# Layer 3's context attention and relative attention as one stage of a Perceiver kernel

## The chip, the core and the metric

The kernel runs on one core of a Trainium2 chip. TensorE (PE) multiplies matrices, VectorE (DVE), ScalarE (ACT) and GpSimd (POOL) work on vectors, and SyncE (SP) issues most DMA transfers. Each engine has its own instruction queue. The metric is the time of one execution in device microseconds. In the profile PE and PEld stand for TensorE's matmuls and weight loads. A float32 matmul appears as two rows of the profile, so a group "x4" is two matmuls.

## The reference, cut to what matters

The whole network is four layers on `x` (2 batches, 256 positions, 256 channels) with a context of 2 x 4096 rows. The change touches two consecutive sublayers of the last layer, each with 16 heads of depth 16 and a residual:

```python
def _L3_xattn_ref(q, kv, mem, w_q, w_kv, w_concat):    # q = layernorm(x), mem = kv = context
    c = jnp.concatenate([mem, kv], axis=1)
    qh = (q @ w_q).reshape(B, L, N_HEAD, D_HEAD).transpose(0, 2, 1, 3)
    kvp = c @ w_kv
    k, v = (kvp[..., :D_HEAD], kvp[..., D_HEAD:])
    attn_score = jnp.einsum('bhid,bjd->bhij', qh, k) / np.sqrt(D_HEAD)
    attn_prob = jax.nn.softmax(attn_score, axis=-1)
    out = jnp.einsum('bhij,bjd->bhid', attn_prob, v)
    return out.transpose(0, 2, 1, 3).reshape(B, L, D) @ w_concat

def _L3_attn_ref(x, gamma, beta, Wq, Wk, Wv, Wr, u_bias, v_bias, Wo, bo, rel_pos_emb):
    xn = (x - mu) * jax.lax.rsqrt(var + EPS) * gamma + beta     # of an x that is normed already
    q, k, v = heads(xn @ Wq), heads(xn @ Wk), heads(xn @ Wv)
    r = (r_emb @ Wr).reshape(2 * L - 1, NUM_HEADS, DEPTH).transpose(1, 0, 2)
    AC = jnp.einsum('bhld,bhmd->bhlm', q + u_bias[None, :, None, :], k)
    BD = jnp.einsum('bhld,hrd->bhlr', q + v_bias[None, :, None, :], r)
    score = (AC + _rel_shift(BD)) / jnp.sqrt(jnp.float32(DEPTH))
    out = jnp.einsum('bhlm,bhmd->bhld', jax.nn.softmax(score, axis=-1), v)
    return out.transpose(0, 2, 1, 3).reshape(B, L, D_MODEL) @ Wo + bo

x = x + _L3_xattn_ref(_layernorm(x), ctx_1024, ctx_1024, ...)
x = x + _L3_attn_ref(_layernorm(x), ...)
```

Batches do not mix in either sublayer. The second sublayer's batch b needs only the first sublayer's batch b, and `r` depends on no activations at all.

## The kernel before

Tokens are held as four tiles of 128 rows (`NT` = 4); tiles 0 and 1 are batch 0, tiles 2 and 3 batch 1. Four heads of 32 rows (16 used, one row for the maximum or the denominator) stand in the 128 partitions of one column block, so a matmul on one head uses 32 rows of the array, and matmuls of different heads can run side by side.

**Context attention, `l3_xattn`.** Work goes in eight groups, one for each token tile and half of the heads; batch 0 is groups 1 to 4, batch 1 groups 5 to 8. A group has 16 rounds over the 4096 context rows. In a round `weights` (L2446 on) makes the scores of the group's heads against 256 context rows (eight matmuls, L2454) and their exponentials on ACT (four instructions, L2458). Two heads that share 32 rows of the array stand side by side in the columns; such a pair fills one bank and is called a head where banks are counted. `weigh` (L2464 on) multiplies the exponentials of the round before with the values (eight matmuls, L2470) and adds the result to a running sum. Beside them `maxima` (L2418 on) makes the row maxima of the next group (matmuls L2430, reductions on DVE L2434). The maxima run two rounds ahead, so the last 18 rounds (two of group 7 and all 16 of group 8) have none; there the sums are added by DVE (L2475) and not by ACT and POOL. The first group's maxima are made ahead of everything by `four_at_once` (the "quads", L2411 and L2415).

PSUM has eight banks. In this stage a pool gives four to the tag "mm" and four to "tr"; a tag's banks are reused in turn. In the last 18 rounds `weights` takes two heads' banks from "tr" and two from "mm", and `weigh` one from "tr".

At the end of a group `back` (L2483 on) turns the sums, divides by the denominator and writes `z`. After the last group all of `z` is transposed, multiplied with the output weight and added to `x`.

**Relative attention, `l3_attn`.** First comes `rT` (relative embeddings times their weight, eight matmuls of 512 columns), then the norm of the norm, a transpose with gamma and beta, and the front: `query` (a matmul pair per batch and column block, with two biases, L2568 and L2569), `key`, `values`. Work then goes in eight units u, one for each token tile and half of the heads. `relative(u)` makes q times r (eight matmuls of 384 columns in four steps of a pair, L2599), copies it to `bd`, writes `bd` to DRAM and reads it back skewed into `bd_shift` (L2604, L2609). `weights(u)` makes the content scores, four turns of two matmuls (L2624), adds the shifted part and finds the maximum on DVE (L2628), and takes exponentials on ACT (L2632). `turned(u)` transposes the result (L2642), `weigh(u)` multiplies with the values (L2655). Round u holds `relative(u + 3)`, `weights(u)`, `turned(u - 1)` and `weigh(u - 2)`, a step of each in turn; `relative` of units 0 to 2 stands ahead of the rounds with queries and keys.

**The order.** `in_order` (L339 on) ties the instructions of the named engines to the order in which the program issues them: PE, DVE and ACT in `l3_xattn`; PE, DVE, ACT and SP in `l3_attn`. Other engines and the parts outside are placed by the scheduler. Weights come through a ring of four buffers.

## Time and profile before

Three runs took 2503.56, 2503.85 and 2503.92 us (median 2503.85). The profiled execution took 2507.48 us, its span from first to last instruction is 2505.7 us, mean granted clock 0.981.

| stretch of the profiled execution, us | what runs | length, us |
|---|---|---|
| 1837 to 1857 | last keys, layer norm, transposes, query projection of the context attention | 20 |
| 1857 to 1893 | maxima of the first group, four heads at once | 36 |
| 1893 to 2229 | rounds with maxima of the next group, 48 us a group | 336 |
| 2229 to 2267.5 | 18 rounds without maxima | 38.4 |
| 2267.5 to 2309 | last sums, output projection, rT, norms, front of the relative attention | 41.5 |
| 2309 to 2382 | rounds of the relative attention | 73 |
| 2382 to 2393 | output projection, start of the feed-forward sublayer | 11 |
| 2393 to 2506 | feed-forward sublayer with experts | 113 |

Rows of the timeline give a start, a length, the engine, the line, what is written and read with the tile sizes, the number of instructions merged into the row, and in brackets how long the engine had been idle and what ended that. Rows of windows give the window, its length, the busy time and instruction count of each engine, the granted clock of PE as a share of the full one, the share of DMA busy time and the GB/s moved. The span of a pipelined PE row is modelled at its end, so starts of successive rows are the surer measure.

### The profile page before, as it was taken

What the parts mean: (1) busy time and instruction counts of PE and PEld (TensorE: products, weight loads), DVE (VectorE), ACT (ScalarE), POOL (GpSimd) and SP (SyncE); (2) the same over time, 40 slices, a digit from 0 to 9 for tenths busy, and PEclk for the clock granted to TensorE, in tenths of its full rate; (3) what the DMA queues carried; (4) which work ended last, traced back from release to release, by engine and by line L of the source; (5) the groups of instructions that cost most, each with busy time, mean ns of one, the idle gap of its engine ahead of it and who ended that gap; (6) DMA issues with size and microseconds to landing.
All of it is one profiled execution on the core that took longest, in us unless ns stands there. A gap on an engine that the chain in (4) does not pass through costs nothing.

```text
span 2505.7 us, 51321 instructions
## 1 busy us (share of the span) xinstructions
PE 2413.6 (96%) x20499; PEld 1612.5 (64%) x20501; DVE 1691.5 (68%) x3077; ACT 1347.7 (54%) x2556; POOL 912.1 (36%) x856
## 2 busy tenths in 40 slices
PE   8999999999999999999899998999989999999989
PEld 6865477777766666666633465556945666665678
DVE  5555588888877777777669755544268888854642
ACT  3334576666666666666466422432215777785612
POOL 0420066666666666665539412001011222210010
PEclk9999999999999999999999999999988999999989
DMA  8221433333342222222410102125840000003656
GB/s 301 97 95 68 141 99 97 98 98 94 99 130 70 69 70 72 70 69 69 137 49 1 68 22 93 60 76 193 312 152 1 2 2 2 2 2 121 235 238 217
DMA packets 92638, 243.60 MB, mean 97 GB/s; under 512 B 8072, under 2 KB 23248, under 8 KB 81904
## 3 DMA queue, kind: packets, MB, share of 16 engines
q1 hardware_dynamic: 81088, 219.08, 26.2%
q10 hardware_dynamic: 8784, 13.24, 1.4%
q0 software_dynamic: 2528, 8.00, 0.9%
q8 instruction: 162, 2.65, 0.4%
q14 instruction: 76, 0.62, 0.1%
HBM read 206.87 MB, written 33.42 MB: 96 GB/s over the span
## 4 chain that ended last, share of the span: by engine, by line
PE 90%; DVE 5%; ACT 2%; DMA 1%; issue 1%; POOL 0%; SPq 0%; DVEq 0%; ACTq 0%; POOLq 0%
PE ps_tr L1238 15%; PE ps_mm L359 14%; PE ps_mm L1285 10%; PE acc L1332 9%; PE ps_tr L2470 5%; PE ps_mm L2430 5%; PE ps_tr L2454 5%; PE acc L359 3%; PE ps_tr L359 2%; PE acc L563 2%; PE acc L1618 2%; PE ps_mm L823 2%; PE ps_mm L1238 2%; PE ps_tr L839 2%; PE ps_tr L921 2%; DVE mx L2415 1%
## 5 line engine op out<-in xcount | busy, mean ns | idle before, releaser
L1320 POOL TENSOR_TENSOR total<-total,S 128x512 f32<-128x512 f32 x434 | 543.1, 1283 | 227.4 <-ACT S L1309 226.9
L1309 ACT ACTIVATE S<-S 128x512 f32<-128x512 f32 x512 | 304.1, 626 | 209.2 <-DVE S L1306 209.0
L1295 DVE TENSOR_TENSOR most<-ps_mm,most 128x512 f32<-128x512 f32 x448 | 278.1, 683 | 101.1 <-ACT S L1292 101.1
L1306 DVE TENSOR_TENSOR S<-S,ps_dec 128x512 f32<-128x512 f32 x512 | 317.2, 677 | 1.7 <-PE ps_dec L1367 1.7
L2434 DVE TENSOR_REDUCE mx<-ps_mm 128x1 f32<-128x512 f32 x448 | 278.1, 683 | 51.4 <-PE ps_tr L2454 48.2
L1292 ACT COPY S<-ps_mm 128x512 f32<-128x512 f32 x512 | 262.4, 598 | 73.3 <-PE ps_mm L1285 73.1
L2458 ACT ACTIVATE PT<-ps_tr 128x512 f32<-128x512 f32 x476 | 246.7, 601 | 81.7 <-PE ps_tr L2454 79.2
L1238 PEld LDWEIGHTS ps_tr<-w_l1x_wv,ctxT 128*64 128x64 f32 x4096 | 235.5, 137 | 46.3 <-issue 41.7
L1285 PE MATMUL ps_mm<-qT,kT 64*128 64x256 f32 x2048 | 256.6, 389 | 0.7 <-DVE qT L1244 0.7
L1332 PE MATMUL acc<-S,v 128*64 128x256 f32 x2048 | 252.2, 385 | 1.7 <-ACT S L1309 1.0
L1238 PE MATMUL ps_tr<-w_l1x_wv,ctxT 128*64 128x128 f32 x4096 | 248.3, 273 | 0.0
L2454 PE MATMUL ps_tr<-qm,kT 32*128 32x256 f32 x1904 | 239.7, 390 | 0.0
L2430 PE MATMUL ps_mm<-kT,qT 32*128 32x512 f32 x896 | 228.3, 625 | 3.4 <-DVE mx L2415 3.3
L1285 PEld LDWEIGHTS ps_mm<-qT,kT 64*128 64x128 f32 x2048 | 188.5, 186 | 44.5 <-issue 12.2
L1332 PEld LDWEIGHTS acc<-S,v 128*64 128x64 f32 x2048 | 139.5, 136 | 96.3 <-ACT S L1292 33.8
L1238 PE MATMUL ps_tr<-ctxT,w_l1x_wk 128*64 128x512 f32 x800 | 189.6, 593 | 0.0
L2454 PEld LDWEIGHTS ps_tr<-qm,kT 32*128 32x128 f32 x1904 | 172.0, 185 | 16.5 <-issue 6.2
L2479 POOL TENSOR_TENSOR sums<-sums,part 128x256 f32<-128x256 f32 x102 | 73.9, 724 | 249.7 <-ACT part L2478 249.7
L2470 PE MATMUL ps_tr<-PT,v 128*32 128x256 f32 x2048 | 139.4, 385 | 0.0
L2430 PEld LDWEIGHTS ps_mm<-kT,qT 32*128 32x128 f32 x896 | 80.2, 187 | 48.4 <-issue 41.1
L336 DVE COPY v<-ps_tr 128x512 f32<-128x512 f32 x120 | 82.4, 687 | 42.5 <-PE ps_tr L1238 42.5
L1238 PEld LDWEIGHTS ps_tr<-ctxT,w_l1x_wk 128*64 128x64 f32 x800 | 59.7, 137 | 70.5 <-issue 58.9
(582 smaller groups left out, 3845.5 us busy)
## 6 DMA issues: line engine op xcount, KB each, us to landing
ctxT<-in_ctxT SPq DMA_DIRECT2D x144, 512.0 KB, 3.6
w_l2f_gu<-in_l2f_gu SPq DMA_DIRECT2D x16, 1024.0 KB, 7.2
bd_dram<-bd SPq DMA_DIRECT2D x8, 1536.0 KB, 6.5
w_l3f_w<-in_l3f_w SPq DMA_DIRECT2D x11, 1028.0 KB, 8.2
w_l3f_w<-in_l3f_w SPq DMA_DIRECT2D x11, 1024.0 KB, 5.4
ctxT<-in_ctxT SPq DMA_DIRECT2D x8, 1024.0 KB, 7.0
ctx<-in_ctx SPq DMA_DIRECT2D x8, 1024.0 KB, 4.8
ahead_ctx<-in_ctxT SPq DMA_DIRECT2D x8, 1024.0 KB, 7.0
```

Of the source, the lines that this page charges most:

```text
L359: self.nc.tensor.matmul(out, lhsT, rhs, start=i == 0, stop=i == len(pairs) - 1)
L1238: nc.tensor.matmul(ps[part], a[:, part], b, start=k == 0, stop=k == len(pairs) - 1)
L1285: nc.tensor.matmul(banks[hh, i][:, j, :], k[part, ts(2 * i + j, P)], q[u][part, :], start=True, stop=True)
L1295: nc.vector.tensor_tensor(m, ps, m, ALU.max)
L1306: nc.vector.tensor_tensor(t, t, spread[u][:, hh, :].unsqueeze(1).to_broadcast([P, 2, L]), ALU.add)
L1309: nc.scalar.activation(t, t, AF.Exp)
L1320: nc.gpsimd.tensor_add(tot, tot, t)
L1332: nc.tensor.matmul(av[u][part], vs[:, 2 * i + j, part], got[hh, i][:, j, :], start=g % 8 == 0 and i + j == 0, stop=g % 8 == 7 and i + j == 2,)
L2430: nc.tensor.matmul(ps, qT[rows, 2 * half + c, ts(t, P)], kT[rows, ts(j, 512)], start=True, stop=True,)
L2434: nc.vector.tensor_reduce(mx[:, c, r, j : j + 1], ps, AX.X, ALU.max)
L2454: nc.tensor.matmul(ps[:, i, :], kT[rows, ts(2 * u + i, P)], q[rows], start=True, stop=True)
L2470: nc.tensor.matmul(ps[ts(r, 32), :], v[:, 2 * u + i, :], pt[:, i, :], start=i == 0, stop=i == 1)
```

## The change

Both sublayers become one function, `l3_attention`, with the same arithmetic save for the reciprocal square roots of the second norm, which POOL computes as a power of -0.5 in place of ACT's square root and DVE's reciprocal.

- `rT` is made at the start, after the layer norm is issued and ahead of the transposes of its result on PE.
- `in_order` covers PE, DVE, ACT, POOL and SP over both attentions.
- In the last 18 rounds of the context attention PSUM is divided anew: three "mm" banks, four "tr", one "acc". All four heads of `weights` take "tr", `weigh` takes "mm". Each of these rounds also takes two steps of `first_front`: batch 0's output projection and norms (`entered`), its queries, relatives 0 and 1, keys and values, with all copies on DVE. Its 22 steps are used up in 11 rounds.
- The weights for that are loaded, and buffers for it are opened in the memory of batch 0's context keys, at group 5, round 3.
- The rounds of the second attention begin at once after the last group. `second_front` (38 steps: relatives 2 to 7 and batch 1's `entered`, queries, keys and values) runs in rounds 0 to 3, two or three steps for each of the four turns of a round.
- `PT` of the context attention has 14 buffers in place of 16; a relative's write and read-back are issued one directly after the other.

```diff
+        rT = front.tile([P, 4, NT * P], F32, name="rT")
+        with self.in_order(e.PE, e.Activation):
+            for c in range(4):
+                ps = self.bank([P, NT * P])
+                self.mm(ps, [(wr[:, k, ts(c, P)], rel[:, k, :]) for k in range(KC)])
+                nc.scalar.copy(rT[:, c, :], ps)
+            xnT = self.to_T(xn)
...
-            def weigh(t, half, u, pts, vector):
-                ps = self.bank([P, 256], "tr")
+        def weigh(t, half, u, pts, more):
+            ps = self.bank([P, 256], "tr" if more else "mm")
...
+        def power(var, eps, name):
+            v, r = (front.tile([P, 2], F32, name=f"{n}_{name}", tag=f"{n}_{name}", bufs=2) for n in ("var", "pow"))
+            nc.vector.tensor_scalar_add(v, var, eps)
+            nc.gpsimd.tensor_tensor(r, v, minus_half, ALU.pow)
+            return r
+        def entered(b):
+            zT = turn(b, zs[b])
+            yield
...
+            for t in range(2):
+                ps = self.bank([P, D])
+                self.mm(ps, [(zT[:, c, ts(t, P)], weight["wo"][:, c, :]) for c in range(KC)])
+                at = x1[:, 2 * b + t, :]
+                nc.vector.tensor_add(at, ps, x[:, 2 * b + t, :])
+                nc.vector.bn_stats(st[:, t, :], at)
+                nc.vector.bn_aggr(mv[:, t, :], st[:, t, :])
+                yield
+            var = mv[:, :, 1]
+            r = power(var, 1e-5, "in")
+            yield
...
+            nc.vector.tensor_mul(both, var, r)
+            nc.vector.tensor_mul(both, both, r)
+            two = power(both, 1e-6, "out")
+            yield
+            nc.vector.tensor_mul(two, two, r)
+            xn = self.xp.tile([P, NT, D], F32, name="xn", tag="xn")
...
+            yield
+            xnTs[b] = turn(b, xn, "gamma")
+            yield
...
+        def first_front():
+            yield from entered(0)
+            for c in (0, 1):
+                query(0, c, True)
+                yield
+            for _ in relative(0, True):
+                yield
...
+        def second_front():
+            yield from one_after_other(relative(2, False), entered(1))
+            query(1, 0, False)
+            yield
+            query(1, 1, False)
+            yield
+            yield from relative(3, False)
...
+                        if one is None:
+                            self.bank_stack.close()
+                            self.banks(self.bank_stack, "l3a", 3, 4, 1)
+                            one = first_front()
-                            pts = weights(*group, u, [PAIRS[1], PAIRS[0]], ["tr", "mm"])
+                        got = weights(*group, u, [PAIRS[1], PAIRS[0]], ["tr", "tr"])
...
+                    if one is not None:
+                        next(one, None)
+                        next(one, None)
...
+            two = second_front()
+            for u in range(10):
+                self.steps_in_turn(
+                    *([scores(u)] if u < 8 else []), some(two, (2, 3, 3, 3, 2)[u] if u < 5 else 0),
+                    *([weighed(u - 2)] if u > 1 else []), *([turned(u - 1)] if 0 < u < 9 else []),
+                )
```

## The prediction

> **What bounds the kernel now.** I read the timeline first, to cut layer 3 into stages, and then busy time by window for them (window, its length, busy us of PE, PE loads, DVE, ACT and POOL with instruction counts, granted clock, DMA share, GB/s).
>
> ```profile
> 1843.00:1850.00 7.00, 5.90 (x13) 3.20 (x14) 2.25 (x6) 0.83 (x3) 0.56 (x2) 0.53 0.96 344
> 1857.00:1893.00 36.00, 23.03 (x124) 5.94 (x116) 35.53 (x16) 0.00 (x0) 0.00 (x0) 0.79 0.03 12
> ...
> 2229.10:2267.50 38.40, 38.38 (x571) 23.71 (x567) 8.56 (x22) 36.02 (x71) 0.73 (x1) 1.00 0.01 3
> 2267.50:2309.00 41.50, 39.01 (x185) 21.30 (x181) 22.30 (x53) 14.51 (x32) 4.12 (x6) 1.00 0.36 130
> 2309.00:2344.90 35.90, 35.90 (x283) 23.47 (x283) 25.92 (x92) 27.25 (x61) 0.00 (x0) 1.00 0.87 305
> 2344.90:2382.00 37.10, 37.10 (x358) 23.57 (x357) 23.41 (x85) 21.64 (x48) 0.00 (x0) 1.00 0.47 161
> ```
>
> The reader is to see that PE is occupied throughout what is rearranged: 18 rounds without maxima (2229.1 to 2267.5), the front (to 2309), the rounds (to 2382). Moving PE work from one full stage into another gains nothing; only idle time and work run side by side can. The front's 41.5 us hold about 3 us of idle PE (0.52, 0.16, 0.56, 0.63, 0.60 and pieces at 2271.6) and rT's 7.0 us (2277.15 to 2284.12). ACT's 36.0 of 38.4 in the 18 rounds is the second thing to see. One such round, from the timeline:
>
> ```profile
> 2242.64 0.48 PE L2454 MATMUL ps_tr<-qm,kT 32*128 32x256 f32 x2
> 2242.65 0.48 PE L2454 MATMUL ps_mm<-qm,kT 32*128 32x256 f32 x2
> ...
> 2243.72 1.15 PE L2470 MATMUL ps_tr<-PT,v 128*32 128x256 f32 x16
> 2243.86 1.08 ACT L2458 ACTIVATE PT<-ps_tr 128x512 f32<-128x512 f32 x2
> ...
> 2244.84 1.09 ACT L2458 ACTIVATE PT<-ps_mm 128x512 f32<-128x512 f32 x2
> ```
>
> Scores take 1.08, weighting the last round's exponentials 1.08, the period is 2.16. The first exponential starts 1.22 after the first score; the fourth ends 2.07 after the first starts. The next scores start at 2244.80, while two exponentials are still to run: possible because two heads stand in "tr" banks and two in "mm" banks, and both rings have spare ones. From the later rounds, two more rows of the timeline:
>
> ```profile
> 2289.90 0.91 PE L2599 MATMUL ps_tr<-rT,qv 32*128 32x384 f32 x4
> ...
> 2352.30 1.13 PE L2624 MATMUL ps_mm<-kT,qu 32*128 32x256 f32 x4
> ```
>
> A relative pair alone takes 0.84 until the next row starts, a score pair 1.06. Both together, on different row groups, take 1.07 (2311.07 to 2312.14): relatives 3 to 7 cost nothing now.
>
> **Part 1: rT moved to the start of layer 3.** PE is idle from 1840.65 to 1844.06, waiting for the layer norm. rT's first matmul needs a bank that DVE (L2245) frees at 1841.07; its weights, loaded in the layer before, are long there. It ends at 1848.0 and now holds up the transposes. From these to the query projection is 2.13 at the low clock, I take 1.3; the projection 6.9 instead of 9.15, since PE no longer goes cold. Then 0.83 more: first quad at 1857.0 instead of 1856.17, **+0.9** (0 to +4, if the clock stays at 0.53). This pays for rT's 7.0 later, counted in part 3.
>
> **Part 2: the first front in the 18 rounds.** Two edits. First, all four heads now take "tr", which has four banks: each round reuses the banks of the round before. The fourth score matmul waits for the fourth exponential (2.07 after the first starts, hand-over 0.05 as at 2272.82 to 2272.87), and then some 0.8 of the 1.22 from scores to exponential is still to come: 2.12 + 0.8 = **2.92** a round, with PE idle 0.8. No row shows this wait, so bounds: 2.16 if it never binds, 2.07 + 1.22 = 3.3 if nothing overlaps. I take 2.92, as three of the four score matmuls can run early.
>
> Second, two front steps a round. Their PE rows: four transposes 0.55 (2319.50 to 2320.03), the output projection of one token tile 0.9 (a quarter of 2385.33 to 2388.90), a query 1.06 (2290.74 to 2291.80), a relative pair 0.84, and, as four matmuls in a row share one 0.2 of start-up (1.06 less 2 x 0.43), a key pair 1.9 and the values 1.7 to 1.9. A round takes 2.1 plus these, but not less than 2.92. In order of rounds: zT's turning and a projection; a projection; DVE alone; xn's turning and a query; a query and a relative pair; two pairs; a pair and a query; a query and a pair; two pairs; a pair and keys; keys and values. Where a step follows its own input, PE waits: zT's copy, 0.69 + 0.15, in round 1; xn's, 0.48 + 0.15, in round 4. Two relative pairs in one round need four "mm" banks of three, so 0.3 for a DVE copy (0.557). Rounds 1 to 11: 4.4, 3.0, 2.9, 4.4, 4.0, 3.8, 4.0, 4.0, 3.8, 5.0, 6.1 = 45.4. The front is then used up; seven bare rounds at 2.92 add 20.4. Total 65.8 for 38.4: **+27.4** (from 57.8, no waits, to 72.5, bare rounds 3.3 and 0.4 more in the others: +19 to +34). DVE does all copies there; at most 2.7 a round it hides beside PE.
>
> **Part 3: after the last group.** Before, 2271.84 to 2381.98, 110.1. Now rounds start at once, with 38 front steps in rounds 0 to 3.
> Round 0: PE 6.7 (scores 4.24, transposes 0.55, projection 1.8), but DVE 8 x 0.50 for scores, 4 x 0.557, zT 0.69, sums and statistics 2.2: **9.1**.
> Round 1: PE's transposes of xn stand second in the round, and all of the round behind them. In DVE's order xn comes after two score reductions (1.0): four small operations 0.64, between them one POOL power, then xn 2 x 0.42, hand-overs 0.4. No row shows the power on two columns; the smallest POOL row is 0.148, a sum 0.724, I take 0.3 by the small ones: a wait of 3.2 (3.0 to 3.6). Then transposes 0.55 and 0.53; a score pair, two queries, a relative pair and a turning 4.35; three pairs in a turn 3.0 (DVE's 2 x 0.50 + 3 x 0.557 + 0.35); queries again 4.35. With 0.3 until DVE starts in round 0, **16.3**.
> Round 2: scores 4.24, turning 2.1, weighing 1.6, keys 3.6, and ten relative pairs of which only about half a turn's fit beside a score pair: 4.4; **16.0**.
> Round 3: 4.24 + 2.1 + 1.6 + values 1.9 + pairs 1.5 = **11.3**.
> Rounds 4 to 7 as before, 31.8 (2344.89 to 2376.71), the rest 5.3. Sum 89.8 for 110.1: **-20.3** (-26 on PE's rows alone; -15 with half a us more in each of the ten turns that mix pairs and projections).
>
> **Costed at nothing.** SP: bd waits for its eight copies, far for bd's landing (2294.91 to 2299.98), behind them the loads of the output weight and the gate, which wait for PE. Far 2 lands by 9 + 5.1 + 7.9 = 22 after the rounds start, needed at 25.4; far 3 by 35.4, needed at 41.4. If the slack goes, 3 to 4 us. The four weight loads in group 5 come 150 us early. POOL: sums, the pads' and values' clearing (0.95 + 0.21) now in program order, POOL busy 11.2 of 48 us there; a late pad clearing meets DVE's slack of 7.3 us a group (40.7 of 48 from 1954 to 2002). ACT loses two table loads of 1.28, off the path.
>
> **Sum.** 0.9 + 27.4 - 20.3 = **+8.0** on the profiled execution's 2507.48, which stands 3.63 above the median of 2503.85. On the median: **2512**.
>
> [...] The quads' window shows a clock of 0.79 with PE busy 23.0 of 36 us, its gaps about 1 us each, while the 18 rounds show 1.00. [...] Where PE is near 80% busy, as from 1698 to 1710 (9.65 of 12 us), the trace shows 1.00, and PE would be 72% busy in the bare rounds (2.1 of 2.92): I keep 1.00 in the sum and give the drop a rival.
>
> **Rivals.**
> A, the four banks don't bind: exponentials free them in time and bare rounds stay at 2.16. Seven times 0.76 and about 2 in the others go: +1, **2505**. For it: three of the four scores can start early. Against it: the fourth exponential ends 2.07 after the first, scores want the bank sooner.
> B, the granted clock drops in the bare rounds and in rounds 0 and 1, as in the quads. Bare rounds near 3.3 (+2.7), a tenth of the front rounds' 45 (+4), 2 in round 1: +17, **2521**.
> C, the other side: the front vanishes in the waits that the four banks open, 18 rounds at 2.92 = 52.6. Then 0.9 + 14.2 - 20.3 = -5.2, **2498.6**. It decides once the 18 rounds take under 53. Against it: rounds have 0.8 of idle PE each, and front rows of 19.4 need 1.8 in eleven.
> D, relative pairs all run beside scores, as now: 8.7 less, -0.7, **2503**. Against it: three pairs in a turn share row groups with the score pair.
>
> **How the numbers follow.** The forecast, 2509 to 2516, has 0.50; A 0.15, B 0.15, C 0.10, D 0.10. The likeliest is 2512. With every bound at one end the sum would be -7 or +23; the range, 2500 to 2522, leaves out C, the upper part of B and those ends. About 0.2% (5 us) is what a measurement tells from no change: slower 0.62 (nine tenths of the forecast, B, a little of A), same 0.28 (most of A and D, a tenth of the forecast, some of C), faster 0.10 (the rest of C and a little of D).
>
> **What would show it.** Eighteen rounds near 66 us, exponentials starting every 2.9 in the last seven, their banks' scores waiting for ACT; PE gaps of some 3 us at the start of round 1; rounds 0 to 3 near 53. It's wrong if bare rounds stay at 2.16, if front rounds come under 3.3, or if far transfers become the wait of rounds 2 and 3.

## The result and the profile after

The changed kernel takes 2540.84 us (median of four executions: 2539.00, 2539.22, 2542.46 and 2557.20), the kernel before 2503.89 us beside it: a ratio of 1.0162, 95% interval 1.0144 to 1.0180. That is 37 us slower, where 8 slower was forecast and 18 was the end of the range. The profiled execution took 2542.46 us with a span of 2540.7. Executions of one kernel differ in their mean granted clock (0.969 to 0.979 in these four), which is why some medians below stand beside a wide range.

Busy time by window, cut at the stages of the changed kernel (columns as before: window, its length, busy us of PE, PE loads, DVE, ACT and POOL with instruction counts, granted clock, DMA share, GB/s):

```profile
1838.97:1847.27 8.30, 8.01 (x25) 3.90 (x25) 3.20 (x14) 4.32 (x7) 0.31 (x1) 1.00 0.98 359
...
2230.48:2295.99 65.51, 64.02 (x653) 38.17 (x653) 26.44 (x63) 35.62 (x70) 2.14 (x3) 1.00 0.23 82
2299.80:2307.00 7.20, 6.91 (x46) 4.72 (x46) 6.36 (x23) 3.81 (x9) 0.67 (x2) 1.00 0.06 18
2307.00:2332.60 25.60, 19.74 (x74) 12.15 (x71) 13.31 (x42) 10.09 (x22) 4.20 (x6) 0.73 0.46 175
2332.60:2358.85 26.25, 23.34 (x122) 13.54 (x121) 10.41 (x30) 9.52 (x21) 0.00 (x0) 0.74 0.55 200
2358.85:2377.68 18.83, 18.26 (x93) 10.93 (x92) 7.09 (x23) 6.74 (x15) 0.00 (x0) 0.64 0.40 140
2377.68:2411.10 33.42, 32.99 (x265) 20.71 (x264) 19.65 (x77) 18.91 (x43) 0.00 (x0) 1.00 0.34 111
```

The lines are rT, the 18 rounds, and then rounds 0, 1, 2, 3 and 4 to 7 of the second attention. The reader is to see two things. The 18 rounds are as forecast, 65.5 us at full clock. Rounds 1 to 3 are not: 70.7 us for the 43.6 of the working, with a granted clock of 0.64 to 0.74 in a stage that ran at 1.00 before.

| stage | forecast, us | measured, us |
|---|---|---|
| last matmuls of the layer before (L975) to the first quad, against before | +0.9 | +1.5 |
| 18 rounds | 65.8 | 65.5 |
| round 0 | 9.1 | 7.2 |
| round 1 | 16.3 | 25.6 |
| round 2 | 16.0 | 26.3 |
| round 3 | 11.3 | 18.8 |
| rounds 4 to 7 | 31.8 | 33.4 |
| from there to the output projection | 8.7 | 9.6 |

Behind the output projection nothing changed (120.0 us to the end of the span, 120.4 before). The last six rows together are 27.7 us more than forecast (120.9 for 93.2), and that is the miss.

One bare round and what follows on PE in round 1, from the timeline:

```profile
2282.36 2.00 PE L2472 MATMUL ps_tr<-qm,kT 32*128 32x256 f32 x16
2284.28 1.07 PE L2488 MATMUL ps_mm<-PT,v 128*32 128x256 f32 x16
2285.28 2.00 PE L2472 MATMUL ps_tr<-qm,kT 32*128 32x256 f32 x16
...
2312.25 0.48 PE L2534 MATMUL ps_mm<-ident,xn 128*128 128x128 f32 x1 [4.43 <-DVE xn L2574]
...
2314.67 2.07 PE L2638 MATMUL ps_mm<-kTa,qu 32*128 32x256 f32 x4
2316.67 3.78 PE L359 MATMUL ps_mm<-xT,w_l3a_wq 128*128 128x256 f32 x8
...
2325.12 0.92 PE L2611 MATMUL ps_tr<-rT,qv 32*128 32x384 f32 x4 [1.18 <-ACT bd L336]
```

The bare round comes every 2.92 us, as worked out; the wait for the fourth bank doesn't show as idle time but as a row of scores of 2.00 us where it was 1.08. In round 1 PE waits 4.43 us for xn. The row of the score pair behind it takes 2.07 us where it took 1.13, that of two queries 3.78 where it took 2.28: the granted clock is 0.50 there, from 2310.9 to 2321.1. Where a turn takes three relative pairs, the third waits 1.18 us for a "tr" bank that ACT is to empty.

### The profile page after: what moved, and what is told of

Read it like the earlier page. It is cut to its first block, busy times and chain, and to the rows that moved or that the text cites. A ratio compares the mean times of both kernels' runs of the same rounds, so it can differ in the third digit from the quotient of the medians.

```text
span 2540.7 us, 51485 instructions
## 1 busy us (share of the span) xinstructions
PE 2439.1 (96%) x20501; PEld 1625.9 (64%) x20501; DVE 1699.1 (67%) x3091; ACT 1339.6 (53%) x2537; POOL 914.1 (36%) x863
## 4 chain that ended last, share of the span: by engine, by line
PE 89%; DVE 5%; ACT 2%; issue 1%; DMA 1%; POOL 0%; DVEq 0%; ACTq 0%; SPq 0%; POOLq 0%
PE ps_tr L1238 15%; PE ps_mm L359 14%; PE ps_mm L1285 10%; PE acc L1332 9%; PE ps_tr L2472 5%; PE ps_mm L2448 5%; PE ps_tr L2488 4%; PE acc L359 3%; PE ps_tr L359 2%; PE acc L563 2%; PE acc L1618 2%; PE ps_mm L1238 2%; PE ps_tr L921 2%; PE ps_mm L823 2%; PE ps_tr L839 2%; DVE mx L2433 1%
## 5 line engine op out<-in xcount | busy, mean ns | idle before, releaser
L2476 ACT ACTIVATE PT<-ps_tr 128x512 f32<-128x512 f32 x512 | 264.4, 603 | 101.9 <-PE ps_tr L2472 101.7
L2472 PE MATMUL ps_tr<-qm,kT 32*128 32x256 f32 x2048 | 249.4, 391 | 0.9 <-ACT part L2496 0.9
L2472 PEld LDWEIGHTS ps_tr<-qm,kT 32*128 32x128 f32 x2048 | 179.6, 185 | 18.8 <-ACT PT L2476 6.0
L2488 PE MATMUL ps_tr<-PT,v 128*32 128x256 f32 x1744 | 116.7, 385 | 0.0
```

The lines of the kernel that those rows point to most:

```text
L2472: nc.tensor.matmul(ps[:, i, :], kT[rows, ts(2 * u + i, P)], q[rows], start=True, stop=True)
L2476: nc.scalar.activation(pt, ps, AF.Exp, scale=0.25)
```

## What the low clock costs

In windows of 4 us from 2308 to 2376, PE's busy time multiplied by what is missing from a clock of 1.00 adds up to 18.9 us. So of the 27.7 us, by this estimate, 18.9 are PE working at half its clock, and 8.8 are waits and longer turns that the working did not have. The same count for every kernel below, from the first scores of the second attention to its output projection, all in us:

| kernel | stage | lost to low clock | stage without that | PE waits in it |
|---|---|---|---|---|
| after | 120.9 | 18.9 | 102.0 | 11.9 |
| e1 | 125.2 | 26.4 | 98.8 | 10.5 |
| e2 | 130.1 | 34.4 | 95.7 | 7.7 |
| e3 | 117.7 | 22.2 | 95.5 | 7.4 |
| e5 | 135.8 | 43.9 | 91.9 | 2.2 |
| e6 | 134.3 | 40.6 | 93.7 | 4.9 |
| e7 | 119.9 | 30.1 | 89.8 | 6.8 |
| e8 | 113.3 | 27.2 | 86.1 | 4.8 |
| e9 | 115.4 | 28.5 | 86.9 | 4.5 |
| e10 | 113.4 | 27.2 | 86.2 | 4.1 |
| f1 | 109.9 | 0.0 | 109.9 | 3.1 |
| f2 | 94.7 | 6.5 | 88.2 | 2.1 |
| g1 | 90.2 | 0.0 | 90.2 | 3.3 |

Each line is one profiled execution; for e5 and e6 it was the slowest of four (2557.70 and 2559.16 us, the fastest 2536.60 and 2535.28), for f1 the fastest. As waits were removed, the stage without the clock's share got shorter, from 102 to 86 us, and the clock took the gain back. In the profiled execution of e5, with hardly a wait left, it took the most.

## Experiments on the waits

My first theory (W): the waits cost their own length, and they also bring the clock down. Rivals: the dense mixture or the transfers bring it down (D), or PE's work is simply longer (S).

**e1**: two steps of the second front to a turn in place of three.

```diff
-some(two, (2, 3, 3, 3, 2)[u] if u < 5 else 0)
+some(two, (2, 2, 2, 2, 1, 1)[u] if u < 6 else 0)
```

> The changed kernel with the steps of the second batch's front dealt two to a turn in rounds 0 to 3 and one in rounds 4 and 5 (2, 2, 2, 2, 1, 1), where it had 2, 3, 3, 3, 2. Theory W (the 27.7 us missed in part 3 are 6 us of PE waits that were not in the sum, 4.43 on xn and 1.18 and 0.56 on ACT's bd copies, and some 19 us in which PE works at half its clock because of these waits): the waits on bd copies go, xn's turning comes one turn later and its wait falls to 2 to 3 us, so the clock still drops once, in round 1; about 2525 us (2518 to 2532). Rival D (the clock drops because the mixture of relative pairs and projections is dense, or because of the transfers, not because of waits): the clock is 0.5 to 0.8 in the same stretches, 2535 to 2541. Rival S (PE's own work in rounds 1 to 3 is simply longer than I took): within 3 us of 2541.

Measured: 2543.43 us (2542.66 to 2543.99), ratio 1.0160 (1.0143 to 1.0177). The wait for xn went as W had it (2.78 for 4.43); those on bd copies got shorter (0.55 to 0.83 for 1.18) but did not go; the time did not fall. S's number fits, but not its reason: PE's rows are longer because the clock is 0.50. Two windows, the first with xn's wait and what follows, the second behind four waits of 0.8:

```profile
2308.00:2332.00 24.00, 21.26 (x65) 12.29 (x66) 10.93 (x30) 6.84 (x16) 2.57 (x4) 0.52 0.30 110
2360.00:2390.00 30.00, 30.00 (x116) 17.85 (x114) 10.01 (x34) 9.11 (x20) 0.00 (x0) 0.50 0.49 176
```

PE is busy for all 30 us of the second window and the clock stays at 0.50. W as I had put it, with a price in proportion to the waits, is wrong.

**e2**: relative 3, which needs only batch 0, moved between the norm and the turning of xn.

```diff
-yield from one_after_other(relative(2, False), entered(1))
+yield from one_after_other(both_of_first(), entered(1))     # relative 2, then relative 3
...
-yield from relative(3, False)
```

> The changed kernel with relative(3), which needs only the first batch, moved ahead: relative(2) and relative(3) both alternate with the steps of entered(1), the counts stay 2, 3, 3, 3, 2. So pairs of relative(3) and a score pair stand between the norm and the transposes of xn. Theory W: xn's wait of 4.43 falls under 2, round 1 loses 3 us of wait and some 4 of low clock; three pairs to a turn stay in rounds 1 to 3, their waits of 1.18 with them and the cold stretch behind the last of these (2348 to 2372): about 2531 us (2523 to 2537). Rival D: 2537 to 2541, clock unchanged. If 2515 or less, the wait on xn alone set off everything.

Measured: 2551.17 us (2550.61 to 2555.76), ratio 1.0197 (1.0180 to 1.0214): slower than the changed kernel, outside every expectation. A single wait of 0.42 in round 6, for a copy of the accumulator, was followed by a clock of 0.50 up to the end of the rounds:

```profile
2389.51 0.66 PE L2667 MATMUL acc<-PTa,values 128*32 128x128 f32 x8 [0.42 <-DVE zTa L336]
2390.10 1.12 PE L2654 MATMUL ps_tr<-ident,far 128*128 128x128 f32 x4
2391.14 2.07 PE L2638 MATMUL ps_mm<-kTa,qu 32*128 32x256 f32 x4
```

That low clock lasts 34.2 us, from 2389.4 to 2423.6. The changed kernel has the same wait of 0.42 in round 6 and its clock stays at 1.00 there, so the length of the wait alone doesn't decide; what fills the two windows is counted under "Experiments on the order".

**e3**: both edits.

> Both edits together: two steps to a turn, and relative(3) beside the norm. Theory W: no wait of PE above 0.7 us is left in rounds 0 to 5, the granted clock stays at 1.00 from 2300 to 2420, and the stage from the first scores to the output projection takes 94 to 99 us where it took 120.9: about 2516 us (2511 to 2522). Rival D: the clock still falls to 0.5 in stretches without a wait, and the time is 2530 or more.

Measured: 2537.84 us (2517.95 to 2543.65), ratio 1.0121 (1.0072 to 1.0170). The wait for xn is 0.2, four waits on bd copies (0.8 to 1.2) and one of 1.1 are left, and the clock is 0.50 from 2323 to 2337 and from 2354 to 2384. One of four executions took 2517.95 at a mean clock of 0.984, the others 2537 to 2544 at 0.972 to 0.977.

**e4**: part 1 alone, on the kernel before (rT at the start of layer 3, 14 buffers for `PT`).

> The kernel before with part 1 alone: rT's four projections moved to the start of layer 3, everything else as before. rT's 7.0 us (2277.15 to 2284.12 in before) leave the full stage; the start gets 0.9 shorter as in the changed kernel (first quad 1855.23 for 1856.17). Part 1 as measured in the changed kernel: 2503.9 - 7.0 - 0.9 = 2496 us (2494 to 2499). Rival: the front after the context attention waits for the two norms, and rT filled these waits; then PE idles there instead and the gain is 2 us or less: 2501 or more.

Measured: 2504.85 us (2502.43 to 2528.43, ten executions), ratio 1.0014 (0.9993 to 1.0035): the rival held, part 1 alone gains nothing. The 0.9 that the expectation takes off is not part 1's (see Part 1 at the end). The timeline of its front:

```profile
2275.86 3.72 PE L359 MATMUL ps_mm<-w_l3x_wo,zTT 128*128 128x256 f32 x16 [0.16 <-ACT zTT L331]
2283.30 0.30 PE L435 MATMUL ps_tr<-ident,xn 128*128 128x128 f32 x1 [3.72 <-DVE xn L405]
...
2286.84 3.78 PE L359 MATMUL ps_mm<-xT,w_l3a_wq 128*128 128x256 f32 x8 [0.26 <-DVE xT L437]
```

rT stood where PE would otherwise wait for the norm of the norm. With rT gone, PE waits 3.72 there, the granted clock is 0.50 from 2284.2 to 2291.0, and the queries in that stretch take 3.78 for the 2.28 of before. The wait of 4.43 in round 1 of the changed kernel is a wait of the same kind, for the norm of batch 1.

## Experiments on the clock

**e5**: at most one relative pair to a turn, and one other step.

```diff
+its = [others(), pairs()]     # others: entered, queries, keys, values; pairs: relatives 2 to 7
...
+some(two, 1 if u < 6 else 0)
```

> The changed kernel with one relative pair to a turn of relatives 2 to 7 (rounds 0 to 5), and beside it one other step of the second batch's front (entered, queries, keys, values) to a turn as long as there are any. So a turn takes at most one pair's two banks and the turning's one of the four tr banks. Theory C (new): the granted clock falls where PE, doing 32-row matmuls, transposes and weighing, waits some 0.8 us or more in a few us, and it doesn't come back while PE does only such work, however busy it is; so the waits on tr banks (0.8 each, four to five in both kernels with two pairs to a turn) must go, all of them. Then: no PE wait over 0.6 us from the first scores to round 6, clock 1.00, and the stage from the first scores to the output projection is the 73.0 us of before's rounds (2309 to 2382) + 7.1 (turnings, projection, queries of the second batch) - 1.8 (the first batch's keys and values) + 3.3 to the output projection = 81.6 us where it took 120.9: about 2503 us (2499 to 2512). Rival D (dense mixing or the transfers cool it): 2520 or more with stretches at 0.5 in rounds 1 to 4.

Measured: 2541.43 us (2536.60 to 2557.70), ratio 1.0159 (1.0122 to 1.0195). The waits were gone as expected; no row from the first scores on has more than 0.41 until the last transposes. The clock of the profiled execution (2557.70) was worse than ever:

```profile
2303.00:2313.00 10.00, 10.00 (x26) 5.63 (x28) 4.54 (x17) 2.64 (x7) 0.00 (x0) 0.50 0.06 23
2313.00:2323.00 10.00, 9.62 (x39) 6.25 (x34) 6.87 (x27) 4.61 (x12) 4.12 (x6) 0.50 0.40 163
2323.00:2333.00 10.00, 10.00 (x28) 5.19 (x27) 3.84 (x12) 3.72 (x8) 0.00 (x0) 0.50 0.33 105
2333.00:2343.00 10.00, 10.00 (x31) 5.52 (x31) 3.01 (x11) 3.03 (x7) 0.00 (x0) 0.50 0.72 262
2343.00:2359.00 16.00, 16.00 (x53) 8.72 (x52) 4.33 (x13) 4.63 (x10) 0.00 (x0) 0.50 0.01 2
...
2364.00:2388.00 24.00, 24.00 (x193) 14.55 (x192) 13.73 (x46) 13.24 (x30) 0.00 (x0) 1.00 0.60 217
```

PE is busy but for one wait of 0.38 us and stays at a clock of 0.50 for 58.0 us. The clock comes back at 2360.6, behind the first two key projections, which use all 128 rows and columns (128*128, 2356.28 to 2359.99). The DMA share is 0.01 in one cold window and 0.72 in another, so transfers are not it either. This is where my theory changed to what I call F: the granted clock follows how much of the array works, not how long PE is busy.

**e6**: the same, with the first front dealt over all 18 rounds (two steps in four rounds, then one).

> The same, and the first batch's front is dealt over all 18 rounds: two steps in each of the first four, then one, where it had two to a round for eleven rounds and then none. If the 0.8 us that PE waits for the fourth bank in a bare round (period 2.93, PE busy 2.1) can take a front step, fourteen rounds take about 3.2 with their step and the stretch from the start of the 18 rounds to the last of them takes 60 to 63 us for 65.5: 3 to 5 us less than the run with one pair to a turn, about 2499. If every step adds to the 2.93 (the exponentials' chain is lengthened by it), no less: 65 to 70 us and the same time or more.

Measured: 2549.97 us (2535.28 to 2559.16), ratio 1.0176 (1.0139 to 1.0212). The total is the clock's (40.6 us lost in the profiled execution). The part that was asked came out as the first expectation had it: from the first front's output projection to the first scores of the second attention 60.1 us, where it is 65.6 in after and e5. The PE time lost in bare rounds can be filled.

**w1 and w2**: twelve unused matmuls at the start of round 7 of e2, of 128 rows in w1, of 32 rows in w2.

```diff
+if u == 7:
+    ps = self.bank([P, L])
+    for _ in range(12):
+        nc.tensor.matmul(ps, weight["wq"][:, 0, 0:P], xnTs[1][:, 0, :], start=True, stop=True)   # w2: [0:32, ...]
```

> The kernel of e2 (relative(3) beside the norm), whose profile has a granted clock of 0.50 from 2390 to 2420 with PE busy without a gap, with twelve more matmuls of 128 rows by 256 columns, results unused, at the start of round 7 (3.2 us at full clock, 6.4 at half). Theory C (only work that fills the array brings the clock back): the clock is 1.00 from the end of these matmuls on; rounds 7 to 9 lose their cold stretch (some 8 us), so the total is within 4 us of 2551. Rival T (the clock comes back by itself after a fixed time, or with any busy stretch of PE): no difference to the next kernel.

> The same place and the same twelve matmuls, but of 32 rows by 256 columns on one row group: PE is as busy as in w1, with a quarter of the array. Theory C: the clock stays 0.50 until the first full-array work behind round 9, as in e2; total 2551 + 6 = 2557 us. Rival T: as w1.

Measured: w1 2543.11 us (2541.51 and 2544.70), w2 2548.23 us (2545.96 and 2550.51). In both profiled executions the clock was, against e2's, still at 1.00 when these matmuls came, so I could not see whether they bring it back. What I saw is the reverse. In w1 the twelve take 5.34 us at a clock of 1.00, where the expectation had 3.2. w1, then w2, before, during and behind them:

```profile
2388.00:2399.90 11.90, 11.48 (x92) 7.57 (x92) 7.00 (x30) 6.94 (x15) 0.00 (x0) 1.00 0.08 27
2399.90:2405.20 5.30, 5.30 (x25) 4.42 (x24) 0.41 (x1) 0.00 (x0) 0.00 (x0) 1.00 0.00 0
2405.20:2412.00 6.80, 6.80 (x60) 3.99 (x59) 3.35 (x14) 3.66 (x8) 0.00 (x0) 1.00 0.01 2
```

```profile
2392.27:2395.00 2.73, 2.73 (x23) 2.24 (x16) 1.95 (x7) 0.91 (x2) 0.00 (x0) 1.00 0.00 0
2395.00:2398.50 3.50, 3.50 (x14) 2.91 (x14) 0.00 (x0) 0.00 (x0) 0.00 (x0) 0.80 0.00 0
2398.50:2416.00 17.50, 17.20 (x91) 9.91 (x90) 4.49 (x18) 5.86 (x12) 0.00 (x0) 0.50 0.00 1
```

Behind the first 3.7 us of the matmuls of 32 rows (from 2393.43), with PE busy all the time, the clock went from 1.00 to 0.50, and it stayed there for 20.5 us, beside score pairs, weighing and transposes. In w1, with 128 rows, it stayed at 1.00.

**c1 and c2**: the same pair of tests in the kernel before, at the start of its round 5, where no wait stands anywhere near.

> The kernel before, whose rounds run without a PE wait at a clock of 1.00, with twelve unused matmuls of 32 rows by 256 columns on one row group at the start of round 5 (5.4 us as in w2; PE is busy throughout, nothing waits). Theory F: a quarter of the array over a few us brings the clock down to 0.50 and the rest of the rounds, some 28 us of score pairs, turnings and weighing, stays there until the last transposes and the output projection: a turn takes 3.63 us for 2.00 (as in e2), so 2503 + 5.4 + 17 to 23 = 2525 to 2532 us. Rival (the clock follows PE's waits): 2503 + 5.4 = 2508.5, clock 1.00.

> The same with all 128 rows at the same place: equally long, four times the array. Theory F and the rival: 2503 + 5.4 = 2508.5 us (2507 to 2510), clock 1.00 in the rounds. If this one is cold as well, both theories fall.

Measured: c1 2531.77 us (2530.44 to 2538.60), ratio 1.0108 (1.0091 to 1.0125); c2 2509.79 us (2507.21 to 2515.85, ten executions), ratio 1.0025 (1.0014 to 1.0036). Windows of c1 before its unused matmuls, in their first and last part, and behind them; then of c2 before, during and behind:

```profile
2340.00:2355.88 15.88, 15.88 (x161) 9.87 (x158) 12.18 (x45) 12.73 (x30) 0.00 (x0) 1.00 0.93 318
2355.88:2359.00 3.12, 3.12 (x15) 2.72 (x15) 1.02 (x3) 0.38 (x1) 0.00 (x0) 0.97 1.10 425
2359.00:2361.77 2.77, 2.77 (x9) 2.07 (x9) 0.00 (x0) 0.00 (x0) 0.00 (x0) 0.50 0.88 264
2361.77:2408.00 46.23, 46.23 (x217) 27.06 (x219) 14.76 (x57) 14.90 (x32) 0.00 (x0) 0.50 0.11 36
```

```profile
2333.00:2349.29 16.29, 16.29 (x165) 10.38 (x165) 12.59 (x47) 13.14 (x31) 0.00 (x0) 1.00 0.94 323
2349.29:2354.56 5.27, 5.27 (x26) 4.37 (x24) 1.11 (x3) 0.47 (x2) 0.00 (x0) 1.00 0.97 335
2354.56:2380.00 25.44, 25.44 (x213) 15.96 (x216) 14.57 (x57) 14.17 (x31) 0.00 (x0) 1.00 0.24 78
```

Both kernels add twelve matmuls to the same place, PE is busy for every microsecond of every window, and they differ by 22 us. With all rows the rounds take what they took; with a quarter of them the rest of the rounds runs at 0.50 for 46 us. The rows are all that differs, and both times lie inside the numbers written down for F. In the profiled execution of the kernel before the clock is 1.00 through the same rounds, up to 2393.0.

In the traces the stretches at 0.50, but for the one at the end of the span, last 3.41 us or a whole multiple of it: 10.24, 3.41, 3.41 and 23.89 in the second attention of the changed kernel, 58.0 and 30.7 in e5, 51.2 in c1. In c1 46 us of PE busy without a gap didn't bring the clock back from 0.50.

## Experiments on the order

To see what the change is worth with the clock kept, I counted how much of the array a turn fills, as an estimate from the profile's rows: rows x columns x time of each record, over the turn's time. By the records' times given in the next expectation, a bare round has 16 score and 16 weighing records of 0.057 us each in 2.92 us, 62%; a turn of rounds 6 and 7 has 0.23 of scores, 0.23 of weighing and 0.45 of turning in 2.00 us, 45%; the unused 32-row matmuls fill 25%.

The traces allow a sharper count. Cut all nineteen of them, from 2230 to 2396, into windows of 3.41 us, the length of the shortest stretches above, in step with the changes of the clock, and count each window's records by their times at full clock (an estimate, as above). At a clock of 1.00 all 38 windows behind which it fell are under 39% (2 of the 691 others are), at 0.50 all 27 behind which it rose are over 39% (2 of the 156 others are): 4 windows of 912 are on the wrong side. By PE's busy share the best levels misjudge 22 windows at 1.00 and 27 at 0.50, by rows alone 14 and 23. So in these traces one value, about 39% of the array over one such window, parts the windows both on the way down and on the way up; transposes are counted like other matmuls. In the second attention of the changed kernel the clock falls behind windows of 2, 35, 35 and 39% and comes back behind windows of 45, 50, 46 and 45%. Rounds 6 and 7, at 45% on the mean, have windows of 40%. The wait of 0.42 leaves its window 33% in e2, where the clock falls, and 39% in the changed kernel, where it holds (one of the four). At 0.50 the same turn takes 3.63 us for 2.00 (e2), so its 0.91 fill only 25%, and in e2 the clock is still at 0.50 behind seven such turns (2389.51 to 2416.39).

**e7**: as e5, but the relative pair directly behind the score pair, so that both run on different rows at once.

```diff
-its = [others(), pairs()]
+its = [pairs(), others()]
```

> The kernel with one pair to a turn, but in each turn the relative pair stands directly behind the score pair and the other step behind both (it stood between them). Theory F (the granted clock follows how much of the array PE's work fills, not how long PE is busy): a score pair alone fills a quarter of the rows, beside a relative pair on other rows it takes 1.07 us for both instead of 1.06 and 0.84 one after the other. Counting rows x columns x time from the rows of the profile (score record 0.25 x 0.227 us, relative record 0.25 x 0.34, weighing record 0.25 x 0.113, transpose record 0.113, projection record 0.227), a turn of rounds 0 to 5 fills 53 to 68% of the array, where rounds 6 and 7, which hold a clock of 1.00 with no wait and lose it with one of 0.42, fill 45%. So the clock stays at 1.00 in rounds 0 to 5, and the stage from the first scores to the output projection takes about 82 us: 2503 us (2499 to 2512); in executions where the wait of 0.42 in round 6 cools the end, some 16 more. Rival P (order inside a turn doesn't matter; it is chance): as the run with one pair to a turn, 2537 to 2557.

Measured: 2535.96 us (2530.78 to 2538.93), ratio 1.0117 (1.0091 to 1.0143). F's number is missed by 33 us. The clock held from the start to 2321, where e5's fell at 2303. Then came waits of 1.86 and 2.10 that the expectation lacked. PE's rows name ACT's bd copy; ACT waits for a score reduction on DVE, and DVE for the transfer:

```profile
2361.93 0.42 DVE L2640 CUSTOM_DVE_ANT_0 far<-ps_mm,far 128x256 f32<-128x256 f32 x1 [2.45 <-DMA far<-bd_dram]
```

So the far transfers, costed at nothing, can be late. Whether that comes of the faster rounds or of the order is not separated: e7 also deals the pairs of relative 3 one to a turn, where the changed kernel had up to three. In f1 below, with the changed kernel's order and a clock of 1.00, PE waits for no bd copy, but its rounds are longer by the unused matmuls.

**e8**: e7 with the banks divided anew before the second attention (3, 3 and 2 accumulators).

> The same, with the banks divided anew before the second attention, 3 mm, 3 tr and 2 accumulators, where there were 3, 4 and 1: weighing then doesn't wait for the copy of the accumulator before (0.42 in round 6, 0.99 in round 9). Theory F: no chance of a cold end is left; 0.5 to 1 us for the new division, 1.4 less for the waits: 2502 us (2499 to 2506), all executions within 5 us. Rival P: 2537 to 2557.

Measured: 2534.59 us (2531.71 to 2539.41), ratio 1.0121 (1.0095 to 1.0146). The wait of 0.42 is gone; the new division costs a wait of 0.71, until 2298.72, and the clock falls at 2300.0; relative pairs still wait 1.01 and 1.67 for bd copies. F's number is missed again, by 33 us.

**e9**: e8 with the old banks in the 18 rounds (two heads from "tr", two from "mm"). **e10**: the same with the first front spread.

```diff
-got = weights(*group, u, [PAIRS[1], PAIRS[0]], ["tr", "tr"])
+got = weights(*group, u, [PAIRS[1], PAIRS[0]], ["tr", "mm"])
```

> The same, and the first front's 18 rounds keep the banks of the rounds before (4 mm and 4 tr), the four heads take two of each, the weighing a tr bank. By part 2's working the bare rounds of 2.93 us go to the 2.16 of before: 7 x 0.77 = 5.4 us less; in the front's eleven rounds the front shares four mm banks with two heads, 0 to 3 us more for waits: 2498 us (2495 to 2502). Rival: the front's copies on DVE are late and the heads in mm wait for them; eleven rounds grow by 5 or more and nothing is gained.

> The same, with the first front dealt over 18 rounds (two steps in the first four, then one). With one front bank a round beside two heads in mm nothing waits: 18 rounds x 2.16 + the front's own rows of 19.4 = 58.3, with 1 to 2 us of hand-overs: 5 to 7 less than e8, 2496 us (2493 to 2500). Rival: as in the run with four banks (68.5 spread, 65.5 not), spreading costs 3 us: 2501.

Measured: e9 2529.35 us (2529.02 to 2537.85), ratio 1.0108 (1.0080 to 1.0135); e10 2526.95 us (2525.37 to 2532.07), ratio 1.0094 (1.0070 to 1.0117). From the first front's output projection to the first scores: 66.4 us in e8, 61.4 in e9, 60.1 in e10. So two rings give 4.9 of the 5.4 us expected, spreading 1.3 more; spreading alone, with four banks, gave the same 60.1 in e6 (the 68.5 in e10's expectation is not what this measure gives). But the totals lie 30 us above the expected ones because both have 27 to 29 us of low clock in the second attention.

**f1**: the changed kernel with unused full-array matmuls put into its waits, nine ahead of xn's turning and two ahead of each third step.

```diff
+if n == 3 and i == 2:
+    unused(2)
...
+if b:
+    unused(9)
 xnTs[b] = turn(b, xn, "gamma")
```

> The changed kernel with full-array matmuls, results unused, put only where PE waits: nine in front of the turning of xn (4.1 us at full clock, into the wait of 4.43) and two in front of the third front step of each turn that has three (0.9 us, into the waits of 1.18). The waits themselves, for DVE's xn and for ACT's copies, are left as they are, and the work is more. Theory F (the granted clock follows how much of the array is at work; the waits cost their length, and twice as much again through the clock they bring down): the clock stays at 1.00 in rounds 1 to 3, where PE's 18.8 us of low clock go; some of the twelve pairs of unused matmuls lengthen a turn that didn't wait, 3 to 5 us: 2526 us (2520 to 2531). Rival (the low clock has another cause, the transfers or the relative work): 2541 or more, clock 0.5 to 0.8 from 2312 to 2372.

Measured: 2535.11 us, ratio 1.0139 (1.0116 to 1.0163), in two kinds of execution: 2528.80 and 2529.81 at a mean clock of 0.985, 2540.42 and 2541.25 at 0.978 and 0.979. The profiled one is of the first kind:

```profile
2308.00:2340.00 32.00, 31.65 (x174) 20.93 (x172) 17.06 (x47) 13.70 (x30) 1.92 (x3) 1.00 0.61 216
2340.00:2372.00 32.00, 31.63 (x227) 19.70 (x227) 15.24 (x52) 16.32 (x36) 0.00 (x0) 1.00 0.59 216
```

The kernel does 33 matmuls more, the waits themselves were left as they are, and it gets 12 us faster where the clock holds. So the low clock of rounds 1 to 3 is real time, and with the waits filled it is gone in this execution (18.9 us lost in the changed kernel, 0.0 here). F's range holds for the first kind of execution alone; the other two have a lower mean clock, and where they lose it no trace shows.

**f2**: e10 with relative 2 in the first two turns and later pairs two turns earlier, turnings ahead of weighing, banks 3, 4 and 1, and four unused matmuls in the wait before the new banks.

> The kernel of e10 (one pair to a turn, two rings in the 18 rounds, front spread), whose profile is at full clock from 2314 to 2354 and cold from 2290 to 2300 and from 2355 to 2398, behind a wait on the new banks (0.72) and one of 1.57 that goes back to a far transfer. Here relative 2 takes the first two turns and all later pairs come two turns earlier (a far transfer lands 13 to 14 us after its last pair in that profile, 2304.75 to 2318.1 in e7), queries 0 to 2 follow the turning of xn at once, the turnings of a round stand ahead of the weighing, the banks are 3, 4, 1, and four unused full-array matmuls stand in the wait before the new banks. Theory F: no wait over 0.6 us in rounds 0 to 6, clock 1.00, and e10's 2527 loses half of some 55 us at low clock and 2 us of waits: 2499 us (2495 to 2508). Rival: waits of other kinds take the place of these, and one of over 1 us cools the rest again: 2515 to 2530.

Measured: 2510.84 us (2510.16 to 2514.91), ratio 1.0035 (1.0021 to 1.0049). That lies between F's range and the rival's. No wait over 0.64 is left in the rounds. The clock falls once, at 2304, behind 3.4 us of score pairs and relative pairs that fill 34% of the array by the count in windows (the 43% of the next expectation is too high: the turning in it starts only at 2303.53), and comes back at 2317 behind two queries.

**g1**: f2 with batch 0's values in place of the four unused matmuls, three unused matmuls in the two turns that had none of PE's projections, and one in xn's copy.

> The kernel of f2, which is at 1.00 but for 2303 to 2318, behind 3.4 us of nothing but score pairs, relative pairs and one turning (43% of the array by the count used before). Here the first batch's values stand where the four unused matmuls stood (2 us out of the 18 rounds, 1.9 us of unused work gone), and three unused full-array matmuls stand in turns 3 and 4, whose front steps give PE nothing, and one in xn's copy. Theory F: clock 1.00 from 2290 to the output projection, 16 us at half clock gone: f2's 2510.8 - 8 - 1.9 + 1.4 = 2502.3 us (2499 to 2506), the same as before. Rival: the clock falls at another place and it stays at 2507 or more.

Measured: 2507.59 us (2506.23 to 2515.87, ten executions), ratio 1.0014 (1.0002 to 1.0026). The clock is 1.00 from 2224 to 2396, as F said, and the stage from the first scores takes 90.2 us where the changed kernel's took 120.9. But the median is 5 us above the expectation. The profiled execution (2515.04) was 10 us behind f2's before layer 3's attention had begun: its first quad stands at 1863.92 where f2's stands at 1853.70, and 55 us of low clock lie ahead of it where f2 has 34. The two kernels differ only behind that point; where the other executions lose their time I can't say from it. No kernel of this study is faster than the kernel before.

## Why the prediction was wrong

The direction was right. **Part 2** was right in its mechanism and its size: four banks bind, 2.92 us a bare round, 65.8 forecast and 65.5 measured (eleven rounds with the front 46.5 for 45.4, seven bare ones 19.0 for 20.4), so rivals A and C fell. **Part 1** costs 1.5 us for its +0.9. The first quad stands 0.9 us earlier than before (1855.23 for 1856.17), but the layer before had ended 2.5 us earlier in that execution; counted from its last matmuls the first quad comes after 20.64 us for 19.12, and after 20.64 in e4 too. In the kernel before, then in the changed one:

```profile
1837.05 3.60 PE L975 MATMUL ps_tr<-behind_ctx,ahead_l3x_wk 128*128 128x512 f32 x8
...
1856.17 2.00 PE L2411 MATMUL quad<-kT,qT 32*128 32x512 f32 x16 [0.83 <-issue]
```

```profile
1834.59 3.60 PE L975 MATMUL ps_tr<-behind_ctx,ahead_l3x_wk 128*128 128x512 f32 x8
...
1855.23 2.00 PE L2429 MATMUL quad<-kT,qT 32*128 32x512 f32 x16 [0.83 <-issue]
```

From the first quad to the 18 rounds it takes 2.3 us longer than before; 0.89 of it is a wait on the new banks, which I had not costed, the rest I did not trace.

The step that failed is in **part 3**, rounds 1 to 3: all their PE rows were taken at full clock, by the sentence "I keep 1.00 in the sum and give the drop a rival" ahead of the rivals. The runs showed 0.73, 0.74 and 0.64 there. Of the 27.7 us missed, 18.9 are the low clock. **Rival B** named the drop of the clock, but put it into the bare rounds and rounds 0 and 1, at 17 us in place of the +8, with a chance of 0.15. The bare rounds and round 0 kept their clock; it fell in rounds 1 to 3. I had judged by PE's busy share ("near 80% busy ... the trace shows 1.00"). That is the wrong measure: c1 is 100% busy at 0.50. The bare rounds, with four heads on four row groups, fill 60 to 68% of the array in each window of 3.41 us, and the four windows behind which the clock falls in rounds 1 to 3 fill 2, 35, 35 and 39%, though the busy share of the bare rounds looked like the worse risk. And the price of 17 counted low clock as ending with its cause, where it lasted 3.4 to 23.9 us at a time in the changed kernel and 58.0 in e5, where it ended behind the key projections, of 128 rows.

The rest of part 3, 8.8 us, is terms that were too small. A turn with three relative pairs was put at 3.0; at full clock it takes 4.4 (2322.17 to 2326.55), because ACT's exponentials stand ahead of the bd copies and the third pair waits 1.18 for a bank. The wait for xn was put at 3.2 and came to 4.7 with its second piece (0.25). POOL's power, taken as 0.3 from the small rows, takes 0.69 each, and DVE's work behind it was drawn out while POOL added the bias rows, which the new order puts there:

```profile
2309.99 0.69 POOL L2546 TENSOR_TENSOR pow_out<-var_out,minus_half 128x2 f32<-128x2 f32 x1 [0.67 <-DVE var_out L2545]
2310.64 2.86 POOL L457 TENSOR_TENSOR xb<-xres,row_l3a_bo 128x256 f32<-128x256 f32 x4
```

```profile
2310.72 0.67 DVE L2571 TENSOR_TENSOR pow_out<-pow_out,pow_in 128x2 f32<-128x2 f32 x1 [0.80 <-POOL pow_out L2546]
2311.42 1.51 DVE L2574 TENSOR_SCALAR xn<-xres,bmv,pow_out 128x256 f32<-128x256 f32 x2
```

The same two DVE rows took 0.16 and 0.74 in the first front, where POOL was idle. No run here separates that.

Rival D fell. **Costed at nothing**: far transfers cost nothing in the changed kernel, as said; in e7, with other rounds, they were late. Counting rT's 7.0 as a pure gain hid that rT had covered the norm's wait, which e4 shows (3.72).

## What to carry to other kernels

When work is moved out of a full stage, look at what the moved work was covering, and at what mixture it leaves behind: in the kernel before, projections of 128 rows stood beside the 32-row attention work, and the clock was 1.00 (60 to 80% of the array in every window of 3.41 us from 2297 to 2330, by the count above). Here a stage of narrow matmuls was better judged by how much of the array it fills in each 3.41 us (4 of 912 windows on the wrong side) than by PE's busy share (49) or by the mean of a long stage (45% in rounds 6 and 7, where e2's clock fell behind a window of 33%); in e2 34.2 us at a clock of 0.50, some 17 us lost, followed a wait of 0.42 us in such a stage. Before believing that a wait is worth its length, fill it with unused full-array matmuls: if the kernel gets faster, as f1 did by 12 us where the clock held, the clock is the price.

## What was not expected of the hardware

- PE was busy without a gap for 46 us (c1), and but for 0.38 us for 58.0 (e5), at a granted clock of 0.50.
- Behind 3 to 4 us of twelve matmuls of 32 rows the clock went from 1.00 to 0.50 (c1, w2), with twelve of 128 rows at the same place it stayed at 1.00 (c2); the kernels c1 and c2 differ by 22 us.
- By the estimate from rows, one value parts the windows of 3.41 us in these traces, on the way down and on the way up: about 39% of the array, with 4 of 912 windows on the wrong side. Turns that fill 45% at a clock of 1.00 take 3.63 us for 2.00 at 0.50, fill 25%, and the clock stayed at 0.50 beside them (e2). It came back behind projections of 128 rows (e5 at 2360.6), and also behind transposes and weighing without any projection (e10 at 2397.2, turns of 0.68 in 1.63 us, 42%). Rows times columns times time fits the traces; no run varies rows or columns alone beyond c1 and c2.
- POOL's power on two columns took 0.69 to 0.73 us.
